# A two-layer graph network on one NeuronCore: the graph product with three pairs of chunks instead of two, and h's transpose and sums prepared a stage earlier

## The chip, the cores and the metric

The kernel runs on one NeuronCore of one Trainium2 chip, in one launch. The metric is the device time of an execution in microseconds (us). A time given for a kernel is the median of several runs. A profile is one execution recorded by the hardware profiler, and its times count from its first instruction.

The engines are named as in the profile: PE (TensorE, matrix products), PEld (its weight loads), DVE (VectorE), ACT (ScalarE), POOL (GpSimd) and SP (SyncE, which only issues DMAs).

## The reference

There are 16 batches of x, each 1024 nodes by 256 channels, and one matrix adj of 1024 by 1024. All is float32.

Layer 0, for each batch: `h = relu(layernorm(x))`, and c_adj, the mean of h over the channels. From it A[n, m] = 2 (0.5 - |sigmoid(c_m - c_n) - 0.5|), and the graph product g = h^T (adj * A), 256 x 1024 by way of 1024 nodes. Then q = relu(g * para), k and v = h @ kv_w, and attention with 4 heads of 64 channels over all 1024 nodes. Its output is added to x.

Layer 1: `h = relu(layernorm(x))` again, agg = A_hat @ h with a normalised adj, then a linear layer to 512 channels, a batch norm over all batches, relu, a linear layer back to 256, a second batch norm, and the sum with x.

## The kernel before

The matrices are cut into chunks of 128 rows. A batch goes through four stages, one after the other on PE: attention (scores L688, values L729), the graph product of the next batch (`graph_seven`), the keys and values of the next batch (L636, L447), and the A_hat product and first linear layer of the batch just attended (`linear1_all`, L889 and L995). One round takes 131.67 us. Nearly every product of two matrices is done in the seven block products of the Strassen-Winograd scheme: instead of eight products of half-size blocks, seven, of sums of the blocks.

Everything stands under `tc.manual_schedule`: each engine executes its instructions in exactly the order in which the program writes them, and a semaphore holds it where data or a buffer is not ready. SP's DMAs form such a queue too: one that waits holds all that follow.

In the graph product the weights w_c of chunk c (128 nodes by 1024) are made in two steps. `differences(b, c)` is two ACT instructions (absolute value and tanh, L350 and L353), `masked(b, c)` is one on DVE (L358, the multiplication with adj). Chunks 0 and 1 get their differences, and their masks, within the attention stage. A tile of w lies in the pool `w4`, with 5 buffers, so that w5 needs the buffer of w0, and so on.

In `graph_seven` the first `PLAIN` = 4 chunks are multiplied plainly: 4 products of 128 x 128 by 128 x 512 for each chunk (L474), into two PSUM tiles `gps`. The chunks 4 to 7 form two pairs. A pair is a 256 x 256 block of h with a 256 x 1024 block of w, and takes the seven products m1 to m_7 (L556). Of w they need the differences t1 to t4, each half a row wide (L522 to L534, DVE), and of h the sums s1 to s4 (L506 to L509, DVE). m1, m6 and m5 of both pairs go into one PSUM bank x, and between them x is copied by ACT into a piece of `room` (L589 after m1, L599 after m6, L604 after m5). A product in float32 is two matmul records in the profile.

The order on PE from the pairs on, before: m1(0) m2(0) m1(1), [copy of x], m_7(0) m3(0) m2(1) m6(0) m_7(1) m3(1) m6(1), [copy of x], m4(0) m4(1) m5(0) m5(1), [copy of x].

`turn_h` (L369) transposes h for the keys and values: two DVE transposes into `f_hQ`, and then 32 DMAs of 32 KB on POOL (L376) that put the 32 x 32 blocks in place in `f_hT`. In a `graph_seven` batch these are the first instructions of the stage. On POOL the two reciprocal roots of `norm.invert` (L258) come behind them.

On SP, the last of attention's normalised output is moved in 16 DMAs of 32 KB (`scale`, L797, tile f_att), once in the attention stage for the first half of the nodes and once in the graph stage for the second. After the first 16 follow `load_thirds` (six DMAs of 512 KB, f_t, sums of A_hat for the stage after), the load of para into the tile of the queries (f_qT, 1 MB, L492), the second 16, and the 256 KB of sums of kv_w (L547).

The pool `pp` has 8 buffers with the tag "p" (attention's exponentials, and between two attentions f_t, f_hT and others) and 2 with the tag "acc".

In the A_hat stage, `linear1` calls back between its products: `late` after the product of s2 and the one of s3 have been issued (there `prepare_end` makes h of the batch after next: L264 on DVE and eight L279 on ACT), and `second` when the last one has been issued (`linear1_seven`, whose first DVE instruction is L987).

Of the kernel before, what the change touches and what calls it, by code (L numbers as in the profile page):

```python
# [29 lines left out]
def fast_path(  # L30
# [33 lines left out]

    x1_d = [dram.tile([N, C], F32, tag=f"fx1_{b}", name=f"fx1_{b}") for b in range(B)]
    row_d = [dram.tile([N], F32, tag=f"frow_{b}", name=f"frow_{b}") for b in range(B)]
    w1s_d = dram.tile([P, 4, FC * P // 2], F32, tag="fw1s", name="fw1s")
    kvs_d = dram.tile([P, 4, P], F32, tag="fkvs", name="fkvs")
    t_d = [dram.tile([P, 4, 512], F32, tag=f"ft_{k}", name=f"ft_{k}") for k in range(3)]
# [104 lines left out]
    with ExitStack() as stage:  # L174
# [170 lines left out]
            differences(b, c)  # L345
            masked(b, c)

        def differences(b, c):
            w = w4.tile([P, N], F32, tag="w4", name=f"f_w_{b}_{c}")
            nc.scalar.activation(  # L350
                w, rows[b], AF.Abs, bias=cols[b][:, c : c + 1], scale=0.5 / C
            )
            nc.scalar.activation(w, w, AF.Tanh)  # L353
            ws[b, c] = w

        def masked(b, c):
            w = ws[b, c]
            nc.vector.scalar_tensor_tensor(w, w, 1.0, adj_t[c], ALU.subtract, ALU.mult)  # L358
# [3 lines left out]
        def turn_h(b, queue=nc.gpsimd):  # L362

            hTs[b] = []
            for d in range(CC):
                t = pp.tile([P, 4, NC, 32], F32, tag="acc", name=f"f_hQ_{b}_{d}", bufs=2)
                nc.vector.transpose(  # L369
                    t.rearrange("p k c r -> p c k r"),  # L370
                    hs[b][:, :, ts(d, P)].rearrange("p c (k i) -> p c k i", k=4),
                )
                to = pp.tile([P, N], F32, tag="p", name=f"f_hT_{b}_{d}")
                for a in range(4):
                    for k in range(4):
                        queue.dma_start(  # L376
                            to[ts(k, 32), ts(a, 32 * NC)],
                            t[ts(a, 32), k].rearrange("i c r -> i (c r)"),
                        )
                hTs[b].append(to)  # L380
# [75 lines left out]
                )  # L456
            return copies

        PLAIN = 4

        def graph_seven(b, left, norm, last):

# [14 lines left out]
                            stop=(c == PLAIN - 1),  # L479
                        )  # L480

            turn_h(b)
            differences(b, 2)
            masked(b, 2)
            collect()
            invert()
            differences(b, 3)
            masked(b, 3)
            differences(b, 4)

            qT = big.tile([P, CC, N], F32, tag="qT", name=f"f_qT_{b}")
            nc.sync.dma_start(qT, para_v)  # L492
            spread()
            scale()
            masked(b, 4)
            plain(0)
            differences(b, 5)
            masked(b, 5)
            kT = big.tile([P, CC, N], F32, tag="kT", name=f"f_kT_{b}")
            v = big.tile([P, NC, C], F32, tag="v", name=f"f_v_{b}")  # L500
            room = v.rearrange("p (n k) c -> p n (k c)", n=4)
            pairs_h = h[:, PLAIN:NC, :].rearrange("p (n k) c -> p n k c", k=2)
            a = lambda i, k: pairs_h[:, :, k, ts(i, P)]
            sums_h = ow.tile([P, 4, 2, P], F32, tag="sums", name=f"f_gs_{b}")
            s1, s2, s3, s4 = (sums_h[:, n] for n in range(4))
            nc.vector.tensor_sub(s3, a(0, 0), a(1, 0))  # L506
            nc.vector.tensor_add(s1, a(1, 0), a(1, 1))
            nc.vector.tensor_sub(s2, s1, a(0, 0))
            nc.vector.tensor_sub(s4, a(0, 1), s2)  # L509
            plain(1)  # L510
            differences(b, 6)
            masked(b, 6)

            def part_w(n, k, j):
                return ws[b, PLAIN + 2 * n + k][:, ts(j, 512)]

            t2 = [kT[:, n, 0:512] for n in range(2)]
            t3 = [kT[:, n, 512:N] for n in range(2)]
            t1, t4 = [None] * 2, [None] * 2

            def make_t3(n):
                nc.vector.tensor_sub(t3[n], part_w(n, 1, 1), part_w(n, 0, 1))  # L522

            def make_t1(n):
                t1[n] = part_w(n, 0, 1)
                nc.vector.tensor_sub(t1[n], t1[n], part_w(n, 0, 0))

            def make_t2(n):
                nc.vector.tensor_sub(t2[n], part_w(n, 1, 1), t1[n])
# [3 lines left out]
                t4[n] = part_w(n, 1, 0)  # L533
                nc.vector.tensor_sub(t4[n], t4[n], t2[n])  # L534

            make_t3(0)
            make_t1(0)
            plain(2)
            differences(b, 7)
            masked(b, 7)  # L540
            make_t2(0)
            plain(3)
            hT = hTs.pop(b)
            t23 = pp.tile([P, 2, 512], F32, tag="acc", name=f"f_kt23_{b}", bufs=2)
            rest = pp.tile([P, 2, 512], F32, tag="acc", name=f"f_kt4_{b}", bufs=2)
            sums = rest[:, 1].rearrange("p (n q) -> p n q", n=4)
            nc.sync.dma_start(sums, kvs_d)  # L547
            make_t3(1)
            make_t1(1)
            make_t2(1)  # L550
            x = ps_t.tile([P, 512], F32, tag="t", name=f"f_gpsx_{b}")
            m7 = ps_o.tile([P, 512], F32, tag="o", name=f"f_gps7_{b}")
            c_of = {(d, g): gps[d][:, ts(g, 512)] for d in range(CC) for g in range(NH)}
# [1 line left out]
            def one(ps, left, right, n, more=True, fresh=False):  # L555
                nc.tensor.matmul(  # L556
                    ps,
                    left[:, n, :],
                    right,
                    start=fresh and n == 0,  # L560
                    stop=(n == 1),
                    skip_group_check=more,
                )

            def m1(n):
                one(x, a(0, 0), part_w(n, 0, 0), n, False, True)

            def m2(n):
                one(c_of[0, 0], a(0, 1), part_w(n, 1, 0), n)

            def m3(n):
                one(c_of[0, 1], s4, part_w(n, 1, 1), n)

            def m4(n):
                one(c_of[1, 0], a(1, 1), t4[n], n)

            def m5(n):
                one(x, s1, t1[n], n)

            def m6(n):  # L580
                one(x, s2, t2[n], n)

            def m_7(n):
                one(m7, s3, t3[n], n, False, True)

            m1(0)
            m2(0)
            m1(1)
            nc.scalar.copy(room[:, 0], x)  # L589
            m_7(0)  # L590
            m3(0)
            m2(1)
            make_t4(0)
            make_t4(1)
            m6(0)
            m_7(1)
            m3(1)
            m6(1)
            nc.scalar.copy(room[:, 2], x)  # L599
            m4(0)  # L600
            m4(1)
            m5(0)
            m5(1)
            nc.scalar.copy(room[:, 1], x)  # L604
            add0()
            nc.vector.tensor_add(room[:, 2], room[:, 2], m7)
# [483 lines left out]
                    nc.vector.bn_stats(st1[:, f2 + i, t, :], z[:, i, :])  # L1090
                nc.sync.dma_start(z1_d[t][:, f2 : f2 + 2, :], z)

        def linear1_all(b, h1, thirds, early, late, last, ending=lambda: None, made=None):


            sums = []

            def first():
                early()
                if b + 1 < B:  # L1100
                    sums.append(load_w1_sums(b))

            def second(agg, up):
                if up is None:
                    up = ow.tile([P, 2, 512], F32, tag="oT", name=f"f_u4_{b}", bufs=2)
                linear1_seven(b, agg, sums[0], up, last, ending)

            def very_last(agg, up):

                for f2 in range(0, FC, 2):  # L1110
                    for t in range(2):
                        zs[t, f2] = fetch(t, f2)
                for g in range(NH):
                    linear1_out(b, g, agg[g], [0])
                bn1.invert(0, 2)
                bn1.affine(0, 2)
                linear1_out(b, 0, agg[0], [2])
                relu_on(zs[0, 0], 0)
                linear1_out(b, 1, agg[1], [2])
                bn1.invert(2, 4)  # L1120
                relu_on(zs[1, 0], 0)

            linear1(
                b, h1, thirds, [first, late, second if b + 1 < B else very_last], made
            )
# [106 lines left out]
        with tc.manual_schedule(engines={ENG.PE, ENG.Activation, ENG.DVE, ENG.Pool, ENG.SP}):  # L1232
# [73 lines left out]
            for b in range(B):  # L1306
# [34 lines left out]
                    between[3].insert(0, roots_row)  # L1341
                    between[4] = scale[:3] + between[4] + [scale[3]]
                if b + 1 < B:
                    if 0 < b < B - 2:
                        thirds = load_thirds(b)
                    if b == 0:
                        qkv = graph(b + 1, between)
                        todo = []
                    else:
                        qkv, todo = graph_seven(b + 1, left, norm, b + 2 == B)  # L1350
                    if b == 0:
                        for step in scale[4:]:
                            step()
                        thirds = make_thirds(b)
                if b + 2 < B:
# [2 lines left out]
                        norm.h,  # L1358
                        thirds,
                        lambda: ([step() for step in todo], prepare_start(b + 2)),  # L1360
                        lambda: prepare_end(b + 2),
                        lambda: (prepare_row(b + 2), again(b + 1)),
                    )
                elif b + 1 < B:
                    kept_h = norm.h
# [933 lines left out]
```

## Time and profile before

| what | value |
|---|---|
| median of 3 runs | 2403.06 us (2402.53 to 2403.59) |
| the profiled execution | 2403.7 us, its span from first to last instruction 2401.8 us |
| granted TensorE clock | 0.995 of full speed, mean over the span |
| busy share of the span | PE 98%, DVE 80%, ACT 56%, POOL 13% |
| DMA | 275.78 MB, 115 GB/s in the mean |
| the six f_t, f_qT, f_hT: issue to landing | 7.0 us, 13.2 us, 2.8 us (medians over all batches) |

How to read it: the busy shares are means over stages with different limits. PE's 98% says that at nearly every moment PE had a product to do. The share of DVE is a mean over the attention stage, where it follows ACT, and the graph stage, where it is closer to full. A transfer's time from issue to landing holds the time in which it stands behind others in the same queue.

### The profile page before, as it was taken

To read this page: it belongs to the slowest core of one execution; us is meant where nothing else is said; L and a number is where in the kernel's file an instruction comes from. 1 tells how busy PE (TensorE), PEld (TensorE's weight loads), DVE (VectorE), ACT (ScalarE), POOL (GpSimd) and SP (SyncE) were. 2 spreads that over 40 slices of the span, in tenths; PEclk is the share of its full clock that TensorE was granted. 3 is DMA by queue.
4 is the path that set the end of the run, shared out by engine and by line. 5 is a ranking of instruction groups with operands and counts; after the bars stand their busy time and mean duration, and the time that the engine had idled before them with its cause. 6 is when DMAs were issued, how large, how long until landed. Compare 5 with 4: busy or idle time off the path is not lost.

```text
span 2401.8 us, 24818 instructions
## 1 busy us (share of the span) xinstructions
PE 2364.5 (98%) x7978; PEld 1040.9 (43%) x7978; DVE 1920.9 (80%) x2694; ACT 1346.9 (56%) x1974; POOL 314.7 (13%) x561
## 2 busy tenths in 40 slices
PE   8999999999999999999999999999999999999996
PEld 4443444434343434444343434344443434444445
DVE  6787979696979788797969697887969698757766
ACT  6846555564646455555646465555556465446654
POOL 2030202011020302020210203020202011000000
PEclk9999999999999999999999999999999999999998
DMA  5042423332332414233323324142333122355579
GB/s 188 7 143 62 128 88 110 102 100 68 102 104 68 148 62 135 80 110 105 100 63 107 107 62 146 62 147 69 110 106 107 63 82 65 105 199 189 176 240 379
DMA packets 176411, 275.78 MB, mean 115 GB/s; under 512 B 37648, under 2 KB 121104, under 8 KB 176272
## 3 DMA queue, kind: packets, MB, share of 16 engines
q1 hardware_dynamic: 156112, 241.55, 31.3%
q0 software_dynamic: 15552, 15.77, 2.5%
q10 hardware_dynamic: 4608, 16.78, 1.7%
q8 instruction: 66, 1.08, 0.2%
q14 instruction: 73, 0.60, 0.1%
HBM read 169.35 MB, written 71.10 MB: 100 GB/s over the span
## 4 chain that ended last, share of the span: by engine, by line
PE 97%; DMA 1%; DVE 1%; issue 0%; ACT 0%; SPq 0%; DVEq 0%; ACTq 0%; POOLq 0%; POOL 0%
PE f_s L688 19%; PE f_o L729 19%; PE f_aps L889 16%; PE f_gps L474 8%; PE f_zps L995 6%; PE f_vps L447 4%; PE f_gps L556 4%; PE f_zx L1516 4%; PE f_zm L1516 3%; PE f_gpsx L556 3%; PE f_kpsx L636 2%; PE f_gps L401 2%; PE f_kps L636 1%; PE f_z2ps L1454 1%; PE f_outps L1739 1%; PE f_zps L1077 1%
## 5 line engine op out<-in xcount | busy, mean ns | idle before, releaser
L696 ACT ACTIVATE f_p<-f_s 128x1024 f32<-128x1024 f32 x512 | 477.3, 1046 | 149.1 <-PE f_s L688 149.1
L705 DVE TENSOR_TENSOR f_acc<-f_acc,f_p 128x1024 f32<-128x1024 f32 x384 | 470.5, 1225 | 41.8 <-DVE f_acc L705 1.4
L688 PE MATMUL f_s<-f_qT,f_kT 64*128 64x512 f32 x2048 | 457.1, 596 | 0.0
L729 PE MATMUL f_o<-f_p,f_v 128*64 128x512 f32 x2048 | 453.6, 595 | 0.0
L376 POOL DMA_DIRECT2D f_hT<-f_hQ x480 | 236.7, 500 | 1237.0 <-PE f_gps L474 1161.0
L688 PEld LDWEIGHTS f_s<-f_qT,f_kT 64*128 64x128 f32 x2048 | 190.3, 185 | 264.3 <-ACT f_p L696 118.4
L729 PEld LDWEIGHTS f_o<-f_p,f_v 128*64 128x64 f32 x2048 | 141.3, 137 | 304.4 <-issue 257.0
L474 PE MATMUL f_gps<-f_w,f_h_a 128*128 128x512 f32 x448 | 196.0, 595 | 0.0
L350 ACT ACTIVATE f_w<-f_row,f_col 128x1024 f32<-128x1024 f32 x127 | 147.0, 1158 | 29.6 <-DMA f_row<-frow 26.9
L358 DVE SCALAR_TENSOR_TENSOR f_w<-f_w,f_adj 128x1024 f32<-128x1024 f32 x127 | 152.8, 1213 | 3.8 <-ACT f_w L353 3.8
L353 ACT ACTIVATE f_w<-f_w 128x1024 f32<-128x1024 f32 x127 | 134.3, 1058 | 4.0
L474 PEld LDWEIGHTS f_gps<-f_w,f_h_a 128*128 128x128 f32 x448 | 84.0, 190 | 111.8 <-issue 99.1
L889 PE MATMUL f_aps<-f_ahatT,f_hs 128*128 128x512 f32 x256 | 115.1, 592 | 0.0
L889 PE MATMUL f_aps<-f_ahatT,f_h_b 128*128 128x512 f32 x256 | 113.4, 596 | 0.0
L447 PE MATMUL f_vps<-f_kvw,f_hT 128*128 128x256 f32 x512 | 113.1, 379 | 0.0
L889 PE MATMUL f_aps<-f_t,f_hs 128*128 128x512 f32 x256 | 112.5, 592 | 0.0
L279 ACT ACTIVATE f_h_b<-f_x,f_shift_b,f_rstd_b 128x256 f32<-128x256 f32 x128 | 66.3, 592 | 77.0 <-DVE f_shift_b L264 77.0
L447 PEld LDWEIGHTS f_vps<-f_kvw,f_hT 128*128 128x128 f32 x512 | 97.3, 190 | 20.1 <-issue 7.2
L279 ACT ACTIVATE f_h_a<-f_x,f_shift_a,f_rstd_a 128x256 f32<-128x256 f32 x126 | 73.8, 586 | 51.4 <-DVE f_shift_a L264 51.4
L702 DVE TENSOR_TENSOR f_acc<-f_p,f_p 128x1024 f32<-128x1024 f32 x64 | 76.3, 1192 | 14.8 <-ACT f_p L696 14.8
L756 ACT COPY f_parts<-f_red 32x64 f32<-32x64 f32 x128 | 39.0, 305 | 79.3 <-DVE f_red L721 78.1
L1018 ACT ACTIVATE f_z<-f_zps,f_b 128x512 f32<-128x512 f32 x60 | 38.0, 684 | 75.3 <-PE f_zps L995 75.3
(261 smaller groups left out, 3241.8 us busy)
## 6 DMA issues: line engine op xcount, KB each, us to landing
f_t<-ft SPq DMA_DIRECT2D x84, 512.0 KB, 7.0
fz<-f_z SPq DMA_DIRECT2D x64, 512.0 KB, 9.2
f_x<-in_x_dram SPq DMA_DIRECT2D x31, 1024.0 KB, 7.4
f_zb<-fz SPq DMA_DIRECT2D x42, 512.0 KB, 4.2
f_att<-f_oT SPq DMA_DIRECT2D x512, 32.0 KB, 1.9
fx<-f_x SPq DMA_DIRECT2D x16, 1024.0 KB, 4.4
f_hT<-f_hQ POOLq DMA_DIRECT2D x480, 32.0 KB, 2.8
f_qT<-in_L_gnn_para_dram SPq DMA_DIRECT2D x14, 1024.0 KB, 13.2
```

The source lines that it names most:

```text
L350: nc.scalar.activation(w, rows[b], AF.Abs, bias=cols[b][:, c : c + 1], scale=0.5 / C)
L358: nc.vector.scalar_tensor_tensor(w, w, 1.0, adj_t[c], ALU.subtract, ALU.mult)
L376: queue.dma_start(to[ts(k, 32), ts(a, 32 * NC)], t[ts(a, 32), k].rearrange("i c r -> i (c r)"),)
L447: nc.tensor.matmul(ps[:, i, :], hT[e][:, ts(c4 + i, P)], kvw_t[:, e, C : 2 * C], start=(e == 0), stop=(e == CC - 1),)
L474: nc.tensor.matmul(gps[d][:, ts(g, 512)], h[:, c, ts(d, P)], w[:, ts(g, 512)], start=(c == 0), stop=(c == PLAIN - 1),)
L556: nc.tensor.matmul(ps, left[:, n, :], right, start=fresh and n == 0, stop=(n == 1), skip_group_check=more,)
L688: nc.tensor.matmul(ps[:, e, :], kT[rows_e, pair, ts(m, P)], qT[rows_e, pair, ts(g, 512)], start=True, stop=True,)
L696: nc.scalar.activation(p, ps, AF.Exp)
L705: nc.vector.tensor_add(acc_of[s], acc_of[s], p)
L729: nc.tensor.matmul(o_of[s][e * HD : (e + 1) * HD, :], v[:, m, ts(2 * pair + e, HD)], p[:, e, :], start=(m == 0), stop=(m == NC - 1),)
L889: nc.tensor.matmul(ps, left[:, m, :], right(m), start=not more and m == 0, stop=(m == KH - 1), skip_group_check=more,)
L1516: nc.tensor.matmul(ps, left[:, m, :], right[:, m, :], start=start and m == 0, stop=(m == 1), skip_group_check=not start,)
```

## The change

The number of plain chunks falls to 2, and the chunks 2 to 7 form three pairs. The new order on PE after the two plain chunks: m1(0) m2(0) m3(0) m_7(0) m1(1) m2(1) m4(0) m_7(1) m3(1) m1(2), [copy of x], m6(0) m6(1) m2(2) m_7(2) m3(2) m6(2), [copy of x], m4(1) m4(2) m5(0) m5(1) m5(2), [copy of x]. The third pair's t2 and t3 lie in pieces of `room` that are free until the copies, and w7 lies in a buffer with the tag "acc".

The transposes of h and the sums s1 to s4 are no longer made in the graph stage. They are made one round earlier, in the A_hat stage, when h of that batch has just been written: the sums of the first two pairs in `late`, those of the third and the transposes at the head of `second`. POOL writes them to DRAM (2 and 8 DMAs instead of 32). At the head of the graph stage SP loads them back, after f_qT and before f_t, which `load_more` now issues.

The batches 2 to 15 go through `graph_seven`; the first two are made as before.

```diff
+    hT_d = [dram.tile([CC, P, N], F32, tag=f"fhT_{b}", name=f"fhT_{b}") for b in range(B)]
+    gs_d = [dram.tile([P, 12, P], F32, tag=f"fgs_{b}", name=f"fgs_{b}") for b in range(B)]
...
-        PLAIN = 4
-
-        def graph_seven(b, left, norm, last):
+        PLAIN = 2
+        PAIRS = (NC - PLAIN) // 2
+
+        def h_pairs(b, n0, n1):
+            view = hs[b][:, PLAIN + 2 * n0 : PLAIN + 2 * n1, :].rearrange(
+                "p (n k) c -> p n k c", k=2
+            )
+            return lambda i, k: view[:, :, k, ts(i, P)]
+
+        def pair_sums(b, n0, n1):
+            n = n1 - n0
+            a = h_pairs(b, n0, n1)
+            t = pp.tile([P, 4, 2, P], F32, tag="p", name=f"f_gs_{b}_{n0}")
+            s1, s2, s3, s4 = (t[:, q, :n] for q in range(4))
+            nc.vector.tensor_sub(s3, a(0, 0), a(1, 0))
+            nc.vector.tensor_add(s1, a(1, 0), a(1, 1))
+            nc.vector.tensor_sub(s2, s1, a(0, 0))
+            nc.vector.tensor_sub(s4, a(0, 1), s2)
+            nc.gpsimd.dma_start(
+                gs_d[b][:, 4 * n0 : 4 * n1].rearrange("p (s n) q -> p s n q", s=4), t[:, :, :n]
+            )
+
+        def turn_h_aside(b):
+            for d in range(CC):
+                t = pp.tile([P, 4, NC, 32], F32, tag="p", name=f"f_hQ_{b}_{d}")
+                nc.vector.transpose(
...
+                to = hT_d[b][d].rearrange("(k i) n -> i k n", k=4)
+                for a in range(4):
+                    nc.gpsimd.dma_start(
+                        to[:, :, ts(a, 32 * NC)],
+                        t[ts(a, 32)].rearrange("i k c r -> i k (c r)"),
+                    )
+
+        def graph_seven(b, left, norm, load_more, last):
...
-            turn_h(b)
+            qT = big.tile([P, CC, N], F32, tag="qT", name=f"f_qT_{b}")
+            nc.sync.dma_start(qT, para_v)
+            hT = []
+            for d in range(CC):
+                t = pp.tile([P, N], F32, tag="p", name=f"f_hT_{b}_{d}")
+                nc.sync.dma_start(t, hT_d[b][d])
+                hT.append(t)
+            w7 = pp.tile([P, N], F32, tag="acc", name=f"f_w_{b}_7", bufs=2)
+            rest = pp.tile([P, 2, 512], F32, tag="acc", name=f"f_kt4_{b}", bufs=2)
...
+            sums_h = ow.tile([P, 4, 2, P], F32, tag="sums", name=f"f_gs_{b}")
+            sums_c = rest[:, 0].rearrange("p (s q) -> p s q", s=4)
+            nc.sync.dma_start(sums_h, gs_d[b][:, 0:8].rearrange("p (s n) q -> p s n q", s=4))
+            nc.sync.dma_start(sums_c, gs_d[b][:, 8:12])
+            nc.sync.dma_start(sums, kvs_d)
+            load_more()
...
             differences(b, 2)
+            differences(b, 3)
+            differences(b, 4)
             masked(b, 2)
+            masked(b, 3)
             collect()
             invert()
...
             masked(b, 4)
             plain(0)
             differences(b, 5)
+            make_t3(0)
+            make_t1(0)
+            make_t2(0)
+            spread()
             masked(b, 5)
             plain(1)
             differences(b, 6)
+            differences(b, 7, w7)
+            m1(0)
+            m2(0)
+            make_t4(0)
+            m3(0)
+            m_7(0)
+            m1(1)
+            make_t3(1)
             masked(b, 6)
...
+            m2(1)
+            m4(0)
+            m_7(1)
+            m3(1)
             make_t1(1)
             make_t2(1)
+            scale()
+            masked(b, 7)
+            m1(2)
             nc.scalar.copy(room[:, 0], x)
+            make_t3(2)
+            make_t1(2)
+            make_t2(2)
+            m6(0)
+            m6(1)
+            m2(2)
             make_t4(1)
+            make_t4(2)
+            m_7(2)
+            m3(2)
+            m6(2)
             nc.scalar.copy(room[:, 2], x)
             m4(1)
+            m4(2)
+            for n in range(PAIRS):
+                m5(n)
             nc.scalar.copy(room[:, 1], x)
...
             def second(agg, up):
+                turning()
...
-                        lambda: prepare_end(b + 2),
+                        lambda: (prepare_end(b + 2), pair_sums(b + 2, 0, 2)),
                         lambda: (prepare_row(b + 2), again(b + 1)),
+                        turning=lambda: (pair_sums(b + 2, 2, 3), turn_h_aside(b + 2)),
```

## The prediction

> **What bounds the kernel now.** I read the page first (busy shares, the chain that ended last), then the chain in order of time for one batch in the middle (window 1000 to 1160), then each engine's timeline and the DMA issues there.
>
> From the page, busy time by engine and the chain by engine:
>
> ```profile
> PE 2364.5 (98%) x7978; PEld 1040.9 (43%) x7978; DVE 1920.9 (80%) x2694; ACT 1346.9 (56%) x1974; POOL 314.7 (13%) x561
> ...
> PE 97%; DMA 1%; DVE 1%; issue 0%; ACT 0%; SPq 0%; DVEq 0%; ACTq 0%; POOLq 0%; POOL 0%
> ```
>
> TensorE sets the time, and it hardly ever waits: 37 us of 2401.8 are not PE. So the change can win only what it takes off PE, and every wait that it puts in PE's way costs its full length.
>
> PE's timeline where the graph stage begins (first line), where its pairs begin, and where the next stage begins (start, length, engine, instructions):
>
> ```profile
> 1047.48 14.00 PE L474 MATMUL f_gps<-f_w,f_h_a 128*128 128x512 f32 x32
> 1061.32 1.02 PE L556 MATMUL f_gpsx<-f_w,f_h_a 128*128 128x512 f32 x2
> ...
> 1073.34 7.07 PE L447 MATMUL f_vps<-f_kvw,f_hT 128*128 128x256 f32 x32
> ```
>
> A product is two matmul records. The 16 plain products take 1061.32 - 1047.48 = 13.84 us, 0.865 each; the 14 products of the two pairs take 12.02 us, 0.859 each. Nothing stands between them: 25.86 us.
>
> What DVE, ACT and DMA do in these two stretches (columns: stretch, its length, then busy us of PE, PEld, DVE, ACT, POOL, clock, DMA share, GB/s):
>
> ```profile
> 1047.50:1061.30 13.80, 13.80 (x34) 6.17 (x33) 13.40 (x19) 12.06 (x18) 7.05 (x15) 1.00 0.90 302
> 1061.30:1073.30 12.00, 12.00 (x29) 5.32 (x28) 10.34 (x21) 1.91 (x3) 6.33 (x14) 1.00 0.55 136
> ```
>
> DVE is nearly full, and so are the 16 DMA engines in the first stretch.
>
> **The products.** `PLAIN` goes from 4 to 2: 8 plain products instead of 16, and 21 products in three pairs instead of 14, so 29 for 30. By the rows, 8 x 0.865 + 21 x 0.859 = 24.95 us: 0.91 us less in each of the 14 batches that `graph_seven` makes.
>
> **DVE and ACT in the stage.** Out go two transposes of h (L369, 2.3 us for both) and four sums (L506 to L509, 0.42 each); in come four half-row differences of a third pair (0.69 each, as L522 to L534). DVE work falls by 1.2 us, and the masks are due sooner. I walked it with the rows' steps (mask 1.13, difference 0.68, L762 to L765 1.28) from the end of L742 at 1049.5: w2 is masked at 1050.6, w5 at 1057.4, t4(0) is there at 1058.0, w6 at 1059.9, w7 at 1063.5. Their products come, without any stall, at 1054.4, 1058.7, 1059.6, 1062.1 and 1064.8: 1.0 us to spare or more. ACT makes differences 2 to 4 in its idle time up to 1048.5, and 5 to 7 as buffers come free (plain(0) ends near 1050.9, plain(1) near 1054.4), the last by 1058.9. I cost this at nothing; if the cover is gone, each us that a mask is late is a us of PE.
>
> **The copy of x.** Now m1(2), then `room[:, 0] <- x` on ACT, then m6(0) and m6(1) into x with no product between m1(2) and m6(0). PE works in order, so everything behind m6(0) waits for the copy. Before, m_7(0), m3(0) and m2(1) lay between. The rows, from PE's and ACT's timelines (m1's last product and its copy; then a copy that PE does wait for today, in the key product):
>
> ```profile
> 1063.04 1.02 PE L556 MATMUL f_gpsx<-f_w,f_h_a 128*128 128x512 f32 x2
> 1063.89 1.02 PE L556 MATMUL f_gps<-f_kT,f_gs 128*128 128x512 f32 x2
> 1064.10 0.59 ACT L589 COPY f_v<-f_gpsx 128x512 f32<-128x512 f32 x1 [2.06 <-PE f_gpsx L556]
> ...
> 1083.21 0.59 ACT L658 COPY f_kT<-f_kpsx 128x512 f32<-128x512 f32 x1 [1.22 <-PE f_kpsx L636]
> 1083.84 0.30 PEld L636 LDWEIGHTS f_kpsx<-f_hT,f_kt 128*128 128x128 f32 x2 [0.65 <-ACT f_kT L658]
> ```
>
> The next product could start at 1063.89; the copy ends at 1064.69, the weight load follows 0.04 later, the matmul 0.03 after that, and its first half runs 0.09 long because its weights were not loaded ahead: 1064.76 + 0.09 - 1063.89 = 0.96 us. That alone eats the 0.91. The later copies have two products (1.72 us) or a whole stage of others behind them and cost nothing.
>
> **The sums by way of DRAM.** m3(0), the eleventh product, needs s4 from `sums_h`, which now comes by DMA; PE waits for that landing and holds every later product behind it. It is due at 8 x 0.865 + 2 x 0.859 = 8.64 us after the stage begins. When is it there? SP issues in order, and ahead of it stand the 16 transfers of `f_att`:
>
> ```profile
> 1036.71 11.00 SPq L797 DMA_DIRECT2D f_att<-f_oT  x16
> 1047.82 3.17 SPq L860 DMA_DIRECT2D f_t<-ft  x6
> 1051.04 0.47 SPq L492 DMA_DIRECT2D f_qT<-in_L_gnn_para_dram  x1
> ```
>
> So SP cannot begin before 1047.8; after the change it issues f_qT (1 MB), two f_hT (512 KB each), then `sums_h` (512 KB, not before L721 has let go of its buffer at 1048.9). The sums are the fifth half-megabyte of the queue. Today's six f_t, 512 KB each, show when those land; the DMA issues of the fourth and the fifth of them (last column: us from issue to landing):
>
> ```profile
> f_t<-ft SPq DMA_DIRECT2D x1, 512.0 KB, 7.8
> ...
> f_t<-ft SPq DMA_DIRECT2D x1, 512.0 KB, 9.2
> ```
>
> Issued at 1049.39 and 1050.01, they land at 1057.2 and 1059.2. Over the 13 batches with f_t, the fourth lands 8.9 and the fifth 11.1 us after the stage's first product (the fifth between 10.2 and 12.0). In the way of the fifth were some 0.26 MB of L376's transfers, which are gone: at 0.33 MB/us 0.7 us less. I take 10.4: nearest to the fifth, which has the same bytes ahead of it. The stall is 10.4 - 8.64 + 0.09 for the cold weight load = 1.85 us; bounds 0.35 (landing like the fourth) and 3.4 (like the latest fifth). `sums_c`, f_hT, f_t, the key sums and f_qT are due 8 us or more after they would land. The next `f_att` transfers wait for f_t to land, which puts their end near 1076, against 1081 when L805 needs them.
>
> **What moves into the A_hat stage.** DVE gets 4 x 0.42 and 2 x 1.2 us and four sums of 128 columns (bounds 0.15 and 0.42 each, by a tiny operation and the 256-column one; I take 0.25): 5 us. It idles there 5.3 us before L942, waiting for ACT, and 3.4 before L987; the first sums fit ahead of the one, the rest (3.4) just ahead of the other, and L987's result is not due for 1.9 us. POOL gets 10 DMAs for 32, 0.5 to 0.9 each by L376 and L81: done by about 1117, before the buffers are reused at 1128. It loses 16 us of issue in the graph stage, so L258's 1 us need not queue behind it; ACT's gain there is off the path. Cost nothing, bounds -0.1 and +1 us a batch.
>
> **The sum.** -0.91 + 0.96 + 1.85 = +1.90 us a batch, x14 = 26.6. The profiled execution took 2403.7 (span 2401.8), so 2430.3; the median of the runs is 0.6 lower, so 2430. With the stall's bounds: 14 x 0.4 and 14 x 3.45 give 2409 to 2451.
>
> PE never idles this long inside the loop today; the granted clock is 1.00 in both stretches, and no row prices a pause. The Trainium skill (TensorE: Matmul & The Clock Gate, the section on the HAM clock gate) speaks against any pause: after one idle window of about 3.4 us the clock falls to half, until one busy window has passed. By that page's figures a drop would cost an estimated 1.7 us a batch, 24 us in all, and make 2454; a stall of 1.85 us stays short of such a window.
>
> **Rivals.**
> - The sums arrive in time (not slower). It decides at a landing before 8.55 us: 2.6 MB in 8.5 us need 308 GB/s from the first issue on. For it: the page's last slices move 379 GB/s, and f_qT alone, in the last batch, lands in 5.4 us. Against it: the fourth f_t, with less ahead of it, lands at 8.9. Then -0.91 + 0.96 = +0.05 a batch: 2404, no change. Chance 0.08.
> - The sums arrive in time and PE does not wait for the copy either: 14 x 0.91 off, 2390. L658's row speaks against it. Chance 0.06.
> - The new writes to DRAM (1.75 MB, 1106 to 1118) delay the row of the next batch: `f_row` is made by a transfer issued at 1116.0 that takes 10.2 us, and ACT has 1.9 us to spare after it before its next exponential. It decides at a delay of 1.9 us; at 3 us it adds 1.1 x 13 = 14: 2445, or more with masks that are late. Chance 0.11.
> - The main case, 2409 to 2451: 0.75.
>
> **Numbers.** Forecast 2430. The range is the main case's own, 2409 to 2451, which also takes in most of the third rival; outside lie the first two and some of the tails. A measurement of this kernel tells about 0.2% (5 us) from no change. Faster 0.06, same 0.08 plus the lowest edge of the main case 0.02, slower 0.84.
>
> **What would show it.** Right: PE idle about 1.9 us before the first f_gps product that reads f_gs, ended by the DMA of f_gs, and about 1 us before f_gpsx's fourth product, ended by ACT's copy; 29 products; the A_hat stage still without gaps. Wrong: no DMA among PE's waits in the graph stage, PE waiting for f_w masks instead, or gaps in the first attention step.

## The result, and the profile after

The changed kernel takes 2414.07 us (median of 5, 2411.89 to 2415.73) against 2403.23 us for the kernel before beside it (median of 5, 2402.53 to 2404.89): a ratio of 1.0044, interval 1.0029 to 1.0058. It is slower, by 10.8 us where 26.9 were forecast (2430). The direction and both waits were as forecast; the size was not.

The profiled execution is the shortest of the five: 2411.9 us, a span of 2410.1, a mean granted clock of 0.996. The page's lines of busy time and of the chain:

```profile
PE 2355.6 (98%) x7950; PEld 1030.2 (43%) x7950; DVE 1975.1 (82%) x2806; ACT 1347.2 (56%) x1974; POOL 174.5 (7%) x253
...
PE 79%; DVE 8%; DMA 6%; ACT 3%; SPq 2%; issue 2%; ACTq 0%; DVEq 0%; POOLq 0%; POOL 0%
```

PE has 28 records less: 14 batches by one product of two records. PE's busy time falls by 9 us while the span grows by 8: PE now waits. The chain's share for PE falls from 97% to 79%, and that must not be read as 18% of the time lost. Once the chain meets a wait for a DMA it is followed back through that DMA's queue, and then through the DVE and ACT work of the attention stage, which ran beside a busy PE. The waits tell the size (in total, times, longest):

```profile
PE f_gpsx L576 <- ACT f_v L641: 9.5, 14, 0.7
PE f_gps L576 <- DMA f_gs<-fgs: 5.5, 10, 1.0
```

The first is the copy of x, the second the sums by way of DRAM. Both undercount: a matmul's modelled end lies 0.16 us after the point where the next could have started, and the cold weight load comes on top. Distances between starts tell more. PE's timeline of a batch with a long wait (start, length, engine, instructions):

```profile
652.00 7.13 PE L514 MATMUL f_gps<-f_w,f_h_a 128*128 128x512 f32 x16
658.98 1.02 PE L576 MATMUL f_gpsx<-f_w,f_h_a 128*128 128x512 f32 x2
659.83 1.02 PE L576 MATMUL f_gps<-f_w,f_h_a 128*128 128x512 f32 x2
661.71 1.12 PE L576 MATMUL f_gps<-f_w,f_gs 128*128 128x512 f32 x2 [0.85 <-DMA f_gs<-fgs]
662.67 1.02 PE L576 MATMUL f_gps<-f_kT,f_gs 128*128 128x512 f32 x2
...
667.82 1.02 PE L576 MATMUL f_gpsx<-f_w,f_h_a 128*128 128x512 f32 x2
669.52 1.98 PE L576 MATMUL f_gpsx<-f_kT,f_gs 128*128 128x512 f32 x4 [0.68 <-ACT f_v L641]
...
679.06 3.18 PE L450 MATMUL f_vps<-f_kvw,f_hT 128*128 128x256 f32 x14
```

m2(0) at 659.83 is followed by m3(0) at 661.71 instead of 660.69; with the 0.10 that its first half runs long, the wait on the sums costs 1.12 here. m1(2) at 667.82 is followed by m6(0) at 669.52 instead of 668.68: 0.84, and 0.10 for its cold half. ACT's copy of x starts 1.06 after m1(2), as long as those before did, and now PE waits for it:

```profile
668.88 0.59 ACT L641 COPY f_v<-f_gpsx 128x512 f32<-128x512 f32 x1 [5.34 <-PE f_gpsx L576]
```

The sums' wait differs from batch to batch. Three batches later it is almost gone:

```profile
1057.39 1.02 PE L576 MATMUL f_gps<-f_w,f_h_a 128*128 128x512 f32 x2
1058.29 1.13 PE L576 MATMUL f_gps<-f_w,f_gs 128*128 128x512 f32 x2
```

Only 0.04 and the cold half remain. SP's queue in the batch at 652.00, and the DMA issues of the sums over all batches (median us from issue to landing), show why:

```profile
641.59 11.00 SPq L852 DMA_DIRECT2D f_att<-f_oT  x16
652.70 0.54 SPq L524 DMA_DIRECT2D f_qT<-in_L_gnn_para_dram  x1
653.47 0.87 SPq L528 DMA_DIRECT2D f_hT<-fhT  x2
654.44 0.60 SPq L535 DMA_DIRECT2D f_gs<-fgs  x1
```

```profile
f_gs<-fgs SPq DMA_DIRECT2D x14, 512.0 KB, 7.2
```

The first load is issued 0.7 us after the stage begins, in other batches between 0.5 before it and 0.8 after it, as the 16 f_att let go of SP. The 2.5 MB then land in a nearly fixed rhythm. In the mean over the 13 batches with f_t: f_qT 5.16 us after the stage's first product, the f_hT 6.51 and 7.84, the sums 9.13, between 8.36 and 9.76. The product that needs them is due at 8.64.

Worked out from the starts, the 14 graph stages take 371.8 us against 361.95 before. The stage without any wait takes 25.00 (below), so this is 14 x 25.00 for the products, 14 x 0.94 for the copy and 8.6 for the sums, 0.6 a batch. The two spans differ by less than these 9.9 us, by 8.3, mostly because the first of these stages begins at 255.94 instead of 257.10. That is no part of the change: with the same work up to there as the kernel before, three of the kernels below begin it at 255.7, 256.1 and 256.3.

In the A_hat stage the moved work found the idle time that was expected (DVE's timeline):

```profile
1106.76 0.43 DVE L478 TENSOR_TENSOR f_gs<-f_h_a 128x256 f32<-128x256 f32 x1 [3.10 <-ACT f_h_a L281]
...
1110.31 0.28 DVE L478 TENSOR_TENSOR f_gs<-f_h_a 128x128 f32<-128x128 f32 x1
...
1111.36 2.36 DVE L490 STREAM_TRANSPOSE f_hQ<-f_h_a 128x1024 f32<-128x1024 f32 x2
```

Sums of 0.43, small sums of 0.28, two transposes of 1.18 each; PE's products there run on without a gap that was not there before.

### The profile page after: what moved, and what is told of

It is laid out like the page before. It is cut to its first block, busy times and chain, and to the rows that moved or that the text cites. A ratio compares the mean times of both kernels' runs of the same rounds, so it can differ in the third digit from the quotient of the medians.

```text
span 2410.1 us, 24462 instructions
## 1 busy us (share of the span) xinstructions
PE 2355.6 (98%) x7950; PEld 1030.2 (43%) x7950; DVE 1975.1 (82%) x2806; ACT 1347.2 (56%) x1974; POOL 174.5 (7%) x253
## 3 DMA queue, kind: packets, MB, share of 16 engines
q8 instruction: 65, 1.06, 0.2%
## 4 chain that ended last, share of the span: by engine, by line
PE 79%; DVE 8%; DMA 6%; ACT 3%; SPq 2%; issue 2%; ACTq 0%; DVEq 0%; POOLq 0%; POOL 0%
PE f_aps L944 16%; PE f_s L743 13%; PE f_o L784 13%; PE f_gps L576 6%; PE f_zps L1050 6%; PE f_vps L450 5%; PE f_gpsx L576 4%; PE f_zx L1588 4%; DVE f_acc L760 4%; DMA f_gs<-fgs 3%; PE f_zm L1588 3%; PE f_kpsx L691 2%; PE f_gps L404 2%; ACT f_p L751 2%; PE f_kps L691 1%
## 5 line engine op out<-in xcount | busy, mean ns | idle before, releaser
L260 POOL TENSOR_TENSOR f_rstd_b<-f_var_b,f_mhalf 128x4 f32<-128x4 f32 (+1 forms) x31 | 33.2, 1071 | 1516.4 <-DVE f_var_b L259 1516.4
L514 PE MATMUL f_gps<-f_w,f_h_a 128*128 128x512 f32 x224 | 99.9, 599 | 0.0
L576 PE MATMUL f_gps<-f_w,f_h_a 128*128 128x512 f32 x168 | 81.2, 592 | 0.0
L776 DVE TENSOR_REDUCE f_red<-f_sums 128x32 f32<-128x1024 f32 x64 | 78.1, 1220 | 2.2
```

What stands on the lines that cost most here:

```text
L576: nc.tensor.matmul(ps, left, right, start=fresh and n == 0, stop=(n == PAIRS - 1), skip_group_check=more,)
```

## The experiments

The theory after the result: the whole loss is two waits of PE, about 0.94 us a batch for the copy and 0.6 to 0.8 for the sums, against 0.9 us a batch of products saved; nothing that moved to the A_hat stage costs anything. The rivals: a cost of the moved work itself, or of the traffic to DRAM, that the waits only seem to explain.

**The sums first in the queue.** Changed kernel, with the load of the sums ahead of f_qT and f_hT:

```diff
+            sums_h = ow.tile([P, 4, 2, P], F32, tag="sums", name=f"f_gs_{b}")
+            nc.sync.dma_start(sums_h, gs_d[b][:, 0:8].rearrange("p (s n) q -> p s n q", s=4))
             qT = big.tile([P, CC, N], F32, tag="qT", name=f"f_qT_{b}")
             nc.sync.dma_start(qT, para_v)
...
-            sums_h = ow.tile([P, 4, 2, P], F32, tag="sums", name=f"f_gs_{b}")
-            nc.sync.dma_start(sums_h, gs_d[b][:, 0:8].rearrange("p (s n) q -> p s n q", s=4))
```

> The changed kernel with one line moved: SP loads the sums of the first two pairs before f_qT and f_hT instead of after them. Theory (each batch pays 0.94 us for the copy of x, and what the sums' landing is later than 8.64 us, and gains 0.91): the sums are then the first half-megabyte in the queue and land 5 to 6 us after the stage begins, PE no longer waits for them, the graph stage is 25.9 us in all 14 batches, and the time is that of the kernel before within 2 us: 2402 to 2405. Rival (late masks or the work moved into the A_hat stage cost the time): it stays at 2411 to 2416.

It took 2404.23 us (11 runs) against 2402.98, ratio 1.0003 (0.9994 to 1.0012). The sums land 3.6 us after their issue, 5.2 after the stage begins, and of the two waits one is left:

```profile
f_gs<-fgs SPq DMA_DIRECT2D x14, 512.0 KB, 3.6
```

```profile
PE f_gpsx L576 <- ACT f_v L641: 9.5, 14, 0.7
```

All 14 stages take 25.94 us. So the wait for the sums is what the changed kernel loses against this one: 10.8 - 1.25 = 9.6 us, 0.69 a batch by the medians, give or take some 0.3 by the two intervals.

**The copy covered.** Changed kernel, with m1(2) and its copy two products earlier:

```diff
             m4(0)
+            m1(2)
+            nc.scalar.copy(room[:, 0], x)
             m_7(1)
             m3(1)
...
-            m1(2)
-            nc.scalar.copy(room[:, 0], x)
```

> The changed kernel with m1(2) and its copy two products earlier on PE, ahead of m_7(1) and m3(1), so that these run while ACT copies x. Theory: PE no longer waits for the copy, 0.94 us less in each of 14 batches, 13 us: about 2401; the wait for the sums stays. Rival (m1(2) then waits for the mask of chunk 6, or another wait takes the copy's place): no gain, 2411 to 2416.

It took 2399.23 us (11 runs), ratio 0.9982 (0.9973 to 0.9991). No product waits for the copy; the sums still cost up to 1.3 us a batch (stages of 25.00 to 26.26).

**Both.**

> Both edits of the other two runs together. Theory: both waits are gone and what is left is the product saved, 0.91 us x 14 = 12.7 us under the kernel before: 2388 to 2392. Rival (without the wait for the sums PE reaches m1(2) before chunk 6 is masked, due 12.4 us into the stage against 12.9): up to 0.5 us a batch is given back, 2395 to 2398.

It took 2390.13 us (5 runs), ratio 0.9944 (0.9930 to 0.9958), and beats both kernels. The chain is PE's again, and neither place has a gap (page, then PE's timeline, then ACT's):

```profile
PE 97%; DVE 1%; DMA 1%; ACT 0%; issue 0%; SPq 0%; DVEq 0%; ACTq 0%; POOLq 0%; POOL 0%
```

```profile
655.96 1.02 PE L576 MATMUL f_gps<-f_w,f_h_a 128*128 128x512 f32 x2
656.81 1.02 PE L576 MATMUL f_gps<-f_w,f_gs 128*128 128x512 f32 x2
...
661.11 1.02 PE L576 MATMUL f_gpsx<-f_w,f_h_a 128*128 128x512 f32 x2
661.96 1.02 PE L576 MATMUL f_gps<-f_kT,f_gs 128*128 128x512 f32 x2
662.82 1.02 PE L576 MATMUL f_gps<-f_w,f_gs 128*128 128x512 f32 x2
663.68 1.88 PE L576 MATMUL f_gpsx<-f_kT,f_gs 128*128 128x512 f32 x4
```

```profile
662.16 0.59 ACT L635 COPY f_v<-f_gpsx 128x512 f32<-128x512 f32 x1 [2.50 <-PE f_gpsx L576]
```

The copy ends at 662.75, still under the first of the two products that now stand between, and m6(0) starts on time at 663.68. Every stage takes 25.00 us against 25.85, and a round 130.74 against 131.67: the product saved is worth 0.93 us a batch, 0.85 in the stage and most of the rest in the key products, where a weight load comes sooner.

**The moved work alone.** Kernel before, with only the transposes made in the A_hat stage and brought back by DRAM; `PLAIN` stays 4:

```diff
-            turn_h(b)
+            hT = []
+            for d in range(CC):
+                t = pp.tile([P, N], F32, tag="p", name=f"f_hT_{b}_{d}")
+                nc.sync.dma_start(t, hT_d[b][d])
+                hT.append(t)
+            load_more()
...
+                        turning=lambda: turn_h_aside(b + 2),
```

> The kernel before with only the transposes of h moved into the A_hat stage and by way of DRAM (f_hT loaded before f_t); four plain chunks, two pairs and the sums in the graph stage stay as before. Theory: the moved work is covered on every engine, 2402 to 2405. Rival: the work in the A_hat stage, or the writes to DRAM, cost 0.3 us or more a batch: 2407 and more. It also tells why the sums landed 1.3 us earlier than estimated: if the f_t transfers were held up by POOL's 32 small transfers or by the transposes, they now land 1.28 us apart; if by how f_t lies in DRAM, still 1.7 to 2.0.

2403.17 us (10 runs), ratio 1.0000 (0.9991 to 1.0009), and a round of 131.67 as before. The rival falls: two transposes on DVE, 8 DMAs on POOL, 1 MB written and 1 MB read a batch cost nothing that shows where they lie. The sums, which this kernel leaves in the graph stage, are in the first experiment, and there nothing but the copy's wait is left either.

**The copy uncovered in the kernel before.** Only the order of these calls:

```diff
             m2(0)
-            m1(1)
-            nc.scalar.copy(room[:, 0], x)
             m_7(0)
             m3(0)
             m2(1)
+            m1(1)
+            nc.scalar.copy(room[:, 0], x)
```

> The kernel before (two pairs, four plain chunks) with m1(1) and its copy of x moved behind m_7(0), m3(0) and m2(1), so that no product stands between m1(1) and m6(0). Theory: PE waits 0.94 us for the copy in each of 14 batches, 13 us: about 2416, with the gap before f_gpsx's third product. Rival (the changed kernel's gap there comes of its third pair or its t2, not of the copy): 2402 to 2405.

2416.70 us (4 runs) against 2403.02, ratio 1.0056 (1.0039 to 1.0073): 0.98 us for each of the 14 batches. Every stage takes 26.80 us, 0.95 more than before:

```profile
1070.23 1.02 PE L556 MATMUL f_gpsx<-f_w,f_h_a 128*128 128x512 f32 x2
1071.93 0.70 PE L556 MATMUL f_gpsx<-f_kT,f_gs 128*128 128x512 f32 x1 [0.68 <-ACT f_v L592]
```

So the copy's price is that of the order, with no third pair and no traffic to DRAM about.

**Why the six f_t were a poor ruler.** The forecast took the sums' landing from the fourth and fifth f_t of before. In their order they land 1.27, 1.97, 1.35, 2.01 and 1.95 us after one another (medians over 13 batches), while in the changed kernel the two f_hT and the sums, 512 KB each, land 1.28, 1.28 and 1.29 after the load ahead of them. Two kernels, each run once (the steps are still medians over 13 batches), ask what slows the third, the fifth and the sixth. First, each f_t in a DRAM tile of its own, so that it is read as one piece and not as 4 KB out of every 8:

```diff
-    t_d = [dram.tile([P, 4, 512], F32, tag=f"ft_{k}", name=f"ft_{k}") for k in range(3)]
+    t_d = [
+        [dram.tile([P, 2, 512], F32, tag=f"ft_{k}_{i}", name=f"ft_{k}_{i}") for i in range(2)]
+        for k in range(3)
+    ]
```

> The kernel before with each of the six f_t in a DRAM tile of its own (512 KB without gaps) instead of two halves to a tile (rows of 4 KB at a pitch of 8 KB). If the pitch slowed the f_t on which the estimate of the landing was built, they now land 1.28 us apart, as the new transfers do; if not, every second one still comes 1.7 to 2.0 us after the one ahead of it. The time is that of the kernel before either way, 2402 to 2405.

2402.87 us. The steps are 1.27, 1.29, 1.28, 1.72 and 1.96: the third f_t is cured (its mean is still 1.52), the fifth in part, the sixth not. The first two land sooner too, in the mean 3.88 and 5.15 us after the stage begins instead of 4.30 and 5.57, and the fifth at 9.73 instead of 11.06. Second, `turn_h`, with its 32 small DMAs on POOL, after the mask of chunk 5:

```diff
-            turn_h(b)
             differences(b, 2)
...
             masked(b, 5)
+            turn_h(b)
```

> The kernel before with turn_h (transposes and POOL's 32 transfers) called after the mask of chunk 5, some 10 us later. If these held up the six f_t, the f_t now land 1.28 us apart; if not, as before. f_hT comes late, so PE waits before the values' product: slower than before by 3 to 12 us a batch, 2440 to 2570.

2423.99 us. The steps are 1.30, 1.92, 1.27, 1.32 and 1.29: now the fifth and sixth are cured and the third is not, and the fifth lands at 10.21. So two things made the f_t late: how they lie in DRAM, and POOL's transfers. The first is not a simple rule. In the experiment with the transposes alone, the same f_t with the same pitch, behind two f_hT, land 1.28 apart, with one slow step of 2.15 to the first of them. And the sums are not read as one piece either: by the code each partition reads 4 KB out of every 6, and they land 1.29 after the load ahead. Why a pitch of 8 KB slows some steps and not all stays open.

The time of this kernel, 21 us more, was expected larger (at least 37): the wait for f_hT before the values' product, on which that was built, did not come. The later masks make m1(1) start about 1.0 us late in each batch, and put little else off:

```profile
1069.82 1.02 PE L556 MATMUL f_gps<-f_w,f_h_a 128*128 128x512 f32 x2
1071.71 1.13 PE L556 MATMUL f_gpsx<-f_w,f_h_a 128*128 128x512 f32 x2 [0.88 <-DVE f_w L358]
```

**The sums last in the queue.** Changed kernel, with the load of the sums behind the six f_t, to see what a long pause of PE does to its clock:

```diff
-            nc.sync.dma_start(sums_h, gs_d[b][:, 0:8].rearrange("p (s n) q -> p s n q", s=4))
             nc.sync.dma_start(sums_c, gs_d[b][:, 8:12])
             nc.sync.dma_start(sums, kvs_d)
             load_more()
+            nc.sync.dma_start(sums_h, gs_d[b][:, 0:8].rearrange("p (s n) q -> p s n q", s=4))
```

> The changed kernel with the sums loaded after the six f_t. Theory (a late landing costs PE its full lateness): they land about 18.7 us after the stage begins, where the last f_t did; the wait grows from 0.6 to 10.1 us, so about 9.5 us a batch in 13 batches (the last one loads no f_t, and stays): 2414 + 124 = 2538. If in addition the clock falls while PE pauses, matmuls are then twice as far apart for a few us, 1 to 2 us a batch more: 2550 to 2565, and a granted clock under 0.99. Rival (the landing of the sums does not set the time): 2411 to 2416.

2567.96 us (2 runs), ratio 1.0685 (1.0664 to 1.0706), 3 us above the range that was expected if the clock falls. PE's timeline around the pause, and four stretches of that batch (columns as before, the eighth the granted clock):

```profile
408.33 1.02 PE L576 MATMUL f_gps<-f_w,f_h_a 128*128 128x512 f32 x2
419.45 2.07 PE L576 MATMUL f_gps<-f_w,f_gs 128*128 128x512 f32 x2 [10.10 <-DMA f_gs<-fgs]
421.32 1.82 PE L576 MATMUL f_gps<-f_kT,f_gs 128*128 128x512 f32 x2
422.97 1.02 PE L576 MATMUL f_gpsx<-f_w,f_h_a 128*128 128x512 f32 x2
```

```profile
400.50:409.00 8.50, 8.50 (x22) 3.72 (x20) 8.33 (x13) 6.55 (x13) 0.00 (x0) 1.00 0.89 324
409.00:419.40 10.40, 0.35 (x1) 0.00 (x0) 9.39 (x12) 3.01 (x3) 0.00 (x0) 0.68 0.94 362
419.40:423.90 4.50, 4.45 (x7) 1.96 (x8) 0.00 (x0) 0.00 (x0) 0.00 (x0) 0.61 0.22 51
423.90:438.00 14.10, 13.43 (x32) 5.74 (x31) 4.97 (x13) 1.17 (x2) 0.30 (x1) 1.00 0.04 9
```

The clock falls within the pause and is 0.61 in the 4.5 us after it: two products take 419.45 to 422.97, 3.52 us instead of 1.72. The pause costs its own length, 10.3 us by the starts, and 1.8 us more; over the 13 batches with such a pause the part beyond its length is 1.5 to 3.0 us, 2.1 in the mean.

## Why the prediction was right in kind and wrong in size

- **The products: right.** Forecast 0.91 a batch off; with both waits gone a round is 0.93 shorter.
- **The copy of x: right.** Forecast 0.96; 0.94 by the starts in every batch, 0.98 by the time of the kernel before with only that order changed. A row of another stage (the key product's copy) gave the price of the same turn from PE to ACT and back.
- **Masks, differences, A_hat stage, POOL, f_row: right.** Forecast nothing. No product of the graph stage waits for a mask, no new gap stands in the A_hat stage or in attention, and the transposes moved alone cost 0.0. The rival of a delayed f_row falls too: its transfer (frow) takes 10.2 us from issue to landing, in the median over the batches, against 11.7 before.
- **The sums by way of DRAM: the step that failed.** The wait was found, with its place, its due time (8.64) and what ends it, but sized at 1.85 us where it is 0.6 in the profiled run and 0.69 by the medians: 14 x (1.85 - 0.69) = 16.2 us, all of the miss. The landing was taken as 10.4 us after the stage's start (the fifth f_t at 11.1, less 0.7 for POOL's transfers; the 0.26 MB at 0.33 MB/us named there make 0.8, and 1 us of the forecast); it is 9.13 in the mean. The correction for POOL was about right: the fifth step of the f_t is 2.14 in the mean against 1.29 in the new queue, 0.85, and with POOL's transfers later the fifth f_t landed 0.85 sooner. What was missing is that the third step was slow as well (2.00 against 1.35 for the queue's counterpart, mean, 0.65) and that the first megabyte landed 0.41 later than it does now (5.57 against 5.16). Both are mostly gone when each f_t has a DRAM tile of its own (1.52 and 5.15), so that the layout, and not two loads in place of one, made the first megabyte late. The row nearest in place was not nearest in kind: layout in DRAM and neighbours in time differed. That the bounds, 0.35 and 3.4, were kept is why 2414 lies in the range, near its low end.
- **A rate was at hand,** as is easily seen afterwards. The second f_t landed 1.27 after the first, 413 GB/s. With four such steps after the first 512 KB at 4.3 the landing would have been 9.4, the wait 0.83 and the forecast 2415. The Trainium skill (DMA: Bandwidth & Descriptors, the section on bandwidth) gives 425 GB/s for a 16 MB load issued from GpSimd; the 512 KB in 1.28 us of SP's queue agree with that within 4%.
- **The rival that they come in time** falls with the rows as they are: 9.13 against 8.55. It needed only another place in the queue, as the first experiment showed; 2404 was its price, and 2404.23 was measured there. The rival in which neither wait is left was priced at 2390, and the kernel with both edits took 2390.13.
- **The clock: it stayed, but at pauses shorter than forecast.** At pauses of up to 1.1 us the granted clock is 1.00 in the stage and 0.996 over the span; a pause of 1.85 us there was never run. That no row prices a pause holds inside the loop only. Near the end of the kernel before, PE pauses for 2.01 us between small products, and soon after it the clock is 0.50 (PE's timeline, then a stretch, columns as before, the eighth the clock):

```profile
2339.21 1.11 PE L1739 MATMUL f_outps<-f_ident,f_z 128*128 128x128 f32 x8 [2.01 <-DVE f_z L1721]
```

```profile
2340.20:2346.90 6.70, 5.84 (x28) 5.71 (x28) 4.80 (x5) 3.10 (x4) 0.00 (x0) 0.50 0.95 339
```

All ten profiles have this pause. In eight the clock then falls to 0.50 for 3.4 to 6.8 us; in two (the sums first, and both edits) it stays at 1.00. The pauses of 1.2 to 1.3 us inside the loop, with `turn_h` later and in the last batch with the sums last, left it at 1.00. So the forecast stall of 1.85 us lay close to a length at which the clock does fall, and that the clock stayed is in part luck: the waits came out shorter. The Trainium skill's rule (TensorE: Matmul & The Clock Gate, the HAM clock gate) names an idle window of about 3.4 us; here 2.01 us were enough in eight executions of ten, so 3.4 us is not a safe length. What a drop costs fits better: 2.1 us a pause in the mean, with the sums last, beside the 1.7 that were estimated from that page.

## What to carry to other kernels

A product saved on a full PE is worth only what its new order leaves uncovered: here one copy without products under it (0.94 us) ate one product (0.93), and two products put between brought all of it back. When work is sent by way of DRAM, ask of its load not how long it takes but when its place in the queue lets it land, and put the load with the nearest due time first; that was worth 10 us here and cost nothing that shows. For a landing that is not in the trace, take the rhythm of undisturbed transfers (the smallest step that repeats) and add for each neighbour, rather than the landing of a transfer that only stands in the same place.

## What the runs showed that was not expected

- Loads of 512 KB, 4 KB to a partition, queued behind one another on SP land 1.28 us apart, again and again. Two causes of longer steps were traced: with 32 KB transfers of POOL alongside 1.7 to 2.0, with 4 KB read out of every 8 KB of DRAM 1.97 in one step of the queue. Others stay open: in the changed kernel, without POOL's transfers, the third and the sixth f_t land 1.63 after the one ahead.
- The wait on the sums costs between nothing and 1.2 us in the batches of one execution with no difference in work, mostly because the first load's issue moves between 0.5 us before the stage and 0.8 after it, with the 16 small transfers ahead of it.
